# Turning the column results of the forward transform on the vector engine instead of the tensor engine

## The chip, the cores and the metric

The kernel runs on one core of one Trainium2 chip. The metric is device microseconds (us) of that core. Everything is computed in fp32.

## What is computed

The input x is 32 images of 32 channels of 128 x 128. Two layers follow each other, each of them "x plus something of the normalised x":

```python
def _gn(v, G=16, eps=1e-5):            # per image, groups of two channels
    g = v.reshape(B_, G, C_ // G, H_, W_)
    m = mean(g, (2, 3, 4)); s = var(g, (2, 3, 4))
    return ((g - m) / sqrt(s + eps)).reshape(v.shape)

# layer 0: five Newton-Schulz steps towards a matrix square root, 1024 matrices of 128 x 128
Y = A / norm(A); Z = I
for _ in range(5):
    T = 0.5 * (3.0 * I - Z @ Y); Y = Y @ T; Z = T @ Z
x = x + Y * sqrt(norm(A))              # A = _gn(x)

# layer 1: a spectral convolution with 32 x 32 modes at two corners
f = fftn(_gn(x), axes=(2, 3)).real
top = einsum('bixy,ioxy->boxy', f[:, :, :32, :32], weights1)
bot = einsum('bixy,ioxy->boxy', f[:, :, -32:, :32], weights2)
x = x + ifftn(zeros with top and bot in place).real
```

The change lies in the forward transform of layer 1, the real part of a two-dimensional Fourier transform cut to 64 rows of modes by 32 columns of modes.

## The kernel before, in words

Layer 0 works on 256 groups of four channels (`b` is the image, `g` the group in it). Each group is a lane, a generator (`newton`, L400) that yields between its steps; up to nine lanes are under way at once, and the main loop (L997) takes one step of each in every round. A step is mostly one set of four products 128 x 128 x 128 on the tensor engine (`products`, L304) into one PSUM bank, and one instruction that takes the bank out: the vector engine for q, v, w, t and xt (`plus`, L282, and L420), the scalar engine for y, m, mb and the final scaling (L276, L416). In most images (`is_far`) the two transposes of v go by the vector engine in 32 x 32 blocks (L373, tile `turn`) and through DRAM; the others go by the tensor engine (`transposed`, L310, against the identity). The eight PSUM banks turn in one pool (`bank`, L147).

Beside the lanes the loop takes steps of other queues: `preps` (statistics of the input), `norms`, `posts`, `specs`, `prods` and `backs` (mode products and inverse transform of images that are through). When a lane ends, `end` (L950) puts into `posts`:

- for each group `settle` (L426): it stores the result, folds columns w and -w into sums and differences on GpSimd (tile `fold`), and takes statistics on the vector engine (L437);
- for every four groups, twice an image and 64 times in all, `forward` (L443): products of the folds with cosines and sines (L455, L461, L467) give the column results of eight channels in one PSUM bank, whose four blocks of 32 partitions are 32 columns of modes, cosine or sine sum, for each of two sets of four channels. The scalar engine copies the bank out (`sw`, L472). In the next step the tensor engine transposes it (four transposes, L313 with tile `sw`), and the scalar engine copies the result, in two halves, into the image's tile `u` (L477), whose partitions are now the rows h;
- once an image `summed` (L485, the normalisation's statistics) and `spectrum` (L514): the row contraction, eight products an image, of 64 rows by 64 modes with 256 columns (L523, accumulated over the two sums s), a copy (tile `z`, L532), four transposes, the scaled spectrum (L541) and its store.

`u` has one buffer. The queue `posts` is stepped once in a round. What the engines' instruction streams look like is then decided by a planner that moves instructions by their readiness, except for those marked `kept`, which keep their order among themselves. At the end, when no lane is left, all queues are stepped without rounds between, and the last image's `forward`, `summed` and `spectrum` stand directly in the chain of work to the end of the kernel.

Of the kernel before, what the change touches and what calls it, by code (L numbers as in the profile page):

```python
# [29 lines left out]
F32 = mybir.dt.float32  # L30
# [6 lines left out]
P = 128  # L37
B = 32
C = 32
G = 16  # L40
# [15 lines left out]
K = 64  # L56
KK = 16
L = 32
# [3 lines left out]
T_FH = slice(64, 192)  # L62
# [6 lines left out]
def conv_preact_kernel(  # L69
# [8 lines left out]
    nc = tc.nc  # L78
# [347 lines left out]
    def settle(b, g, st, xt):  # L426

        kept(nc.sync.dma_start(out=mid[b][:, 4 * g : 4 * g + 4, :], in_=xt))
        if g % 2 == 0:
            folds[b, g // 2] = sets.tile([P, 8, P], F32, tag="fold", name=f"fold{b}_{g}", bufs=3)  # L430
        f = folds[b, g // 2][:, 4 * (g % 2) : 4 * (g % 2) + 4, :]
        for half, op in enumerate((ALU.add, ALU.subtract)):
            nc.gpsimd.tensor_tensor(  # L433
                f[:, :, 64 * half : 64 * half + 64], xt[:, :, 0:64], xt[:, :, 64:128], op
            )
        for j in range(2):
            nc.vector.bn_stats(  # L437
                st[:, 2 * g + j, :], xt[:, 2 * j : 2 * j + 2, :].rearrange("p c h -> p (c h)")
            )
        settled.append(rounds)  # L440
        yield

    def forward(b, q, u):  # L443


        yield
        fs = [folds.pop((b, 2 * q + i)) for i in range(2)]
        ps = bank()
        out = ps.rearrange("p j x -> p (j x)").rearrange("p (c h) -> p c h", h=64)
        cos, sin = (slice(T_FW.start + 32 * i, T_FW.start + 32 * i + 32) for i in range(2))  # L450

        for i in (1, 0):
            rows = slice(64 * i + 32, 64 * i + 64)
            kept(
                nc.tensor.matmul(  # L455
                    out[rows, :, 1:64], tab[:, sin], fs[i][:, :, 65:128], start=True, stop=True
                )
            )
            rows = slice(64 * i, 64 * i + 32)
            kept(  # L460
                nc.tensor.matmul(out[rows], tab[:, cos], fs[i][:, :, 0:64], start=True, stop=True)  # L461
            )

        for i in (1, 0):
            rows = slice(64 * i + 32, 64 * i + 64)
            kept(
                nc.tensor.matmul(  # L467
                    out[rows, :, 0], tab[:, cos], fs[i][:, :, 64], start=True, stop=True
                )
            )  # L470
        sw = sp.tile([P, 4, P], F32, tag="sp", name="sw", bufs=2)
        nc.scalar.copy(sw, ps)  # L472
        yield
        ps = transposed(sw)
        for i in range(2):
            c = 8 * q + 4 * i
            nc.scalar.copy(  # L477
                u[:, :, :, c : c + 4].rearrange("h s l c -> h (s l) c"),
                ps[:, :, 64 * i : 64 * i + 64].rearrange("h c m -> h m c"),
            )  # L480
        yield

    scales = {}
# [1 line left out]
    def summed(b, st):  # L485

        ms, _, d = yield from moments(st, "b")
        yield

        q = small.tile([P, G], F32, tag="b_qs", name=f"b_qs{b}")  # L490
        nc.vector.tensor_reduce(q, d, AX.X, ALU.add)
        qr = small.tile([P, 8, G], F32, tag="b_qr", name=f"b_qr{b}")
        nc.vector.tensor_copy(qr, q[:, None, :].to_broadcast([P, 8, G]))
        mr = small.tile([P, 2, G], F32, tag="b_mr", name=f"b_mr{b}")
        nc.vector.tensor_copy(mr, ms[:, None, :].to_broadcast([P, 2, G]))
        yield from pause
        pv = bank()[:, 0, :]
        nc.tensor.matmul(
            pv[:, 0:1], qr.rearrange("p l g -> p (l g)"), avg_v, start=True, stop=True
        )  # L500
        nc.tensor.matmul(
            pv[0:C, 1:2], mr.rearrange("p c g -> p (c g)"), avg_0, start=True, stop=True
        )
        v = small.tile([P, 2], F32, tag="b_v", name=f"b_v{b}")
        nc.vector.tensor_scalar(v[:, 0:1], pv[:, 0:1], 1.0, EPS, ALU.mult, ALU.add)
        nc.vector.tensor_copy(v[0:C, 1:2], pv[0:C, 1:2])
        yield
        s = root(v[:, 0:1], 1, "b_r", 256.0)
        r = small.tile([P, 1], F32, tag="b_inv", name=f"b_inv{b}")
        nc.vector.reciprocal(r, s)  # L510
        scales[b] = v, r
        yield

    def spectrum(b, u):  # L514


        uv = u.rearrange("h s (t e l) c -> h s e t (l c)", e=2, l=4)
        ps = [bank() for _ in range(2)]
        for s in range(2):
            for i in range(2):  # L520
                for e in range(2):
                    rows = slice(64 * i, 64 * i + 64)
                    nc.tensor.matmul(  # L523
                        ps[i][64 * e : 64 * e + 64, 0:2, :],
                        tab[rows, T_FH.start + s * K : T_FH.start + (s + 1) * K],
                        uv[rows, s, e],
                        start=(s == 0),
                        stop=(s == 1),
                    )
        z = sp.tile([P, 4, P], F32, tag="sp", name="z", bufs=2)  # L530
        for i in range(2):
            nc.scalar.copy(  # L532
                z.rearrange("p t (l i c) -> p (t l) i c", i=2, c=G)[:, :, i, :],
                ps[i].rearrange("p a x -> p (a x)")[:, 0:256].rearrange("p (m c) -> p m c", c=G),
            )
        yield
        v, r = scales.pop(b)
        ps = transposed(z)
        spec = sp.tile([P, 4, P], F32, tag="sp", name=f"spec{b}", bufs=2)
        spec = spec.rearrange("p a x -> p (a x)").rearrange("p (k q t) -> p k q t", q=4, t=8)  # L540
        nc.scalar.activation(  # L541
            spec.rearrange("p k q t -> p t (k q)"),
            ps.rearrange("p t (e k) -> p (t e) k", e=2),
            AF.Identity,
            scale=r,
        )
        nc.vector.scalar_tensor_tensor(  # L547
            spec[0:C, 0, 0, 0:1], v[0:C, 1:2], r[0:C], spec[0:C, 0, 0, 0:1], ALU.mult, ALU.add
        )
        yield  # L550
        i, j = where[b]
        if i == len(xs):

            for e, t in enumerate(diags):
                for l4 in range(4):
                    rows = slice(32 * l4, 32 * l4 + 32)
                    copy = nc.scalar.copy if l4 % 2 else nc.vector.tensor_copy
                    copy(  # L558
                        t.rearrange("p (m b l f) -> p m b l f", b=2, l=4, f=4)[rows, :, j, l4, :],
                        spec[rows, 8 * e : 8 * e + 8].rearrange("p k q (h f) -> p (k q h) f", f=4),  # L560
                    )
            yield
            return
        kept(
            nc.sync.dma_start(
                out=xs[i][:, :, j, :].rearrange("k p m -> p k m"),
                in_=spec.rearrange("p (k e) q t -> p k (e q t)", e=KK // xs[i].shape[0]),
            )
        )
        yield  # L570
# [379 lines left out]
    def end(b, g, xt):  # L950

        if g == 0:
            u = up.tile([P, 2, L, G], F32, tag="u", name=f"u{b}")
            st = small.tile([P, G, 6], F32, tag="b_st", name=f"b_st{b}", bufs=2)
            ended[b] = (u, st)
        u, st = ended[b]
        posts.append(settle(b, g, st, xt))
        if g == C // 4 - 1:
            posts.append(then(summed(b, st)))
        if g % 4 == 3:  # L960
            posts.append(forward(b, g // 4, u))
        if g == C // 4 - 1:
            posts.append(last(b, u))
# [33 lines left out]
    while todo or any(lanes) or posts or specs or prods or backs:  # L997
# [3 lines left out]
        for i in range(LANES):  # L1001
# [5 lines left out]
            if lanes[i] is None and todo and room and rounds >= due:  # L1007
# [3 lines left out]
                b, g = todo.pop(0)  # L1011
# [33 lines left out]
def _table():  # L1045

    import numpy as np

    k = np.concatenate([np.arange(32), np.arange(96, 128)]).reshape(4, KK).T.reshape(K)
    n = _order()  # L1050
    row = 2 * np.pi * (np.outer(n, k) % P) / P
    col = 2 * np.pi * (np.outer(n, np.arange(L)) % P) / P
    t = np.zeros((P, T_COLS))
    t[:, T_FW] = np.concatenate([np.cos(col), np.sin(col)], 1)
    half = np.concatenate([np.cos(row), -np.sin(row)], 1)[0:64]
    half[0] = np.concatenate([k % 2 == 0, k % 2 == 1])
    t[:, T_FH] = np.tile(half, (2, 1))
    half = np.concatenate([np.cos(row)[0:64], np.sin(row)[0:64]])
    half[0], half[64] = k % 2 == 0, -(k % 2)
    t[:, T_IH] = np.tile(half.T, (2, 1))  # L1060
    t[:, T_IW] = np.tile(np.concatenate([np.cos(col).T, np.sin(col).T], 1) / (P * P), (4, 1))
    return t.astype(np.float32)
# [37 lines left out]
```

## Time and profile before

| | |
|---|---|
| three runs of the kernel before | 3098.29, 3114.35, 3108.08 us |
| median | 3108.08 us |
| span of the profiled execution (first to last instruction; the profile states no other time of it) | 3098.6 us |
| TensorE (PE) busy | 2948.7 us, 95% |
| weight loads (PEld) busy | 2828.6 us, 91% |
| VectorE (DVE) busy | 2340.0 us, 76% |
| ScalarE (ACT) busy | 1704.0 us, 55% |
| GpSimd (POOL) busy | 1998.0 us, 64% |
| DMA | 636.78 MB, 206 GB/s over the span |

The profile is of one execution. A group of instructions is one source line on one engine with one pair of tiles; its "busy" counts time that overlaps with its neighbours once, and its "mean ns" is that of one instruction from start to end, so count times mean exceeds busy where instructions overlap. Every fp32 product shows as two MATMUL records: the four products of a lane's step are x8, one set of four transposes is x4. A timeline's second column is the duration of a merged stretch; the difference between the starts of two neighbours on one engine is the slot that the first one takes.

### The profile page before, as it was taken

How to read it: one execution, taken by the hardware profiler on the slowest of the kernel's cores; microseconds unless marked ns; L12 is line 12 of the kernel's file. 1: busy time of each engine (PE TensorE's matmuls, PEld its weight loads, DVE VectorE, ACT ScalarE, POOL GpSimd, SP SyncE). 2: the span in 40 equal slices, each digit the busy share in tenths (PEclk: the TensorE clock that was granted, in tenths of full speed). 3: DMA queues.
4: the chain of work that ended last, by engine and by line, in shares of the span. 5: the costliest groups of instructions: out<-in, count | busy, mean ns of one | idle time of the engine just before them, and what ended most of it. 6: DMA issues, size and time to landing. Idle time of an engine off the chain costs nothing. (4 is left out here: it accounts for less than half of the span.)

```text
span 3098.6 us, 79471 instructions
## 1 busy us (share of the span) xinstructions
PE 2948.7 (95%) x29760; PEld 2828.6 (91%) x29760; DVE 2340.0 (76%) x5178; ACT 1704.0 (55%) x4153; POOL 1998.0 (64%) x2312
## 2 busy tenths in 40 slices
PE   6999999999999999999999999999999998999994
PEld 6899999999999999999999998998899988899983
DVE  6788887888888787788877555788778766878654
ACT  3566556666665665666654444555454544555552
POOL 3567677677776666677665434768677764777453
PEclk9999999999999999999999999999999999999996
DMA  4576676666666666676743466667676876766666
GB/s 130 164 216 207 202 217 211 210 213 214 212 209 208 209 207 183 201 212 208 219 146 100 143 217 214 226 228 235 206 250 209 269 233 211 236 208 204 194 218 221
DMA packets 475150, 636.78 MB, mean 206 GB/s; under 512 B 97040, under 2 KB 255248, under 8 KB 474768
## 3 DMA queue, kind: packets, MB, share of 16 engines
q1 hardware_dynamic: 361872, 425.88, 42.8%
q10 hardware_dynamic: 112896, 205.83, 21.7%
q8 instruction: 237, 3.88, 0.5%
q14 instruction: 145, 1.19, 0.1%
HBM read 402.42 MB, written 229.11 MB: 204 GB/s over the span
## 5 line engine op out<-in xcount | busy, mean ns | idle before, releaser
L388 POOL TENSOR_TENSOR w<-w,r 128x512 f32<-128x512 f32 x288 | 366.3, 1276 | 324.3 <-DMA w<-turn 274.8
L307 PE MATMUL ps<-w,v 128*128 128x128 f32 x4096 | 554.6, 279 | 18.0 <-DVE w L282 7.7
L341 ACT ACTIVATE b<-b,a_off,a_scr 128x128 f32<-128x128 f32 x1024 | 468.7, 490 | 154.6 <-issue 48.1
L307 PE MATMUL ps<-y,q 128*128 128x128 f32 x4096 | 527.0, 277 | 6.2 <-ACT d L893 2.1
L307 PEld LDWEIGHTS ps<-w,v 128*128 128x128 f32 x4096 | 504.0, 194 | 25.1 <-POOL w L388 11.0
L307 PEld LDWEIGHTS ps<-y,q 128*128 128x128 f32 x4096 | 490.5, 193 | 9.6 <-issue 2.6
L433 POOL TENSOR_TENSOR fold<-xt 128x256 f32<-128x256 f32 x512 | 363.8, 731 | 204.5 <-DVE xt L420 192.2
L282 DVE SCALAR_TENSOR_TENSOR q<-ps,eye 128x512 f32<-128x512 f32 x512 | 348.0, 680 | 156.8 <-PE ps L307 151.5
L827 POOL TENSOR_TENSOR yt<-yt,d 128x512 f32<-128x512 f32 x248 | 311.2, 1282 | 153.7 <-ACT d L893 116.0
L301 POOL TENSOR_TENSOR r<-mb,eye 128x512 f32<-128x512 f32 x112 | 142.7, 1274 | 311.3 <-ACT mb L276 298.8
L348 POOL TENSOR_SCALAR x<-xt,a_nm,a_sc 128x128 f32<-128x128 f32 x736 | 322.7, 451 | 19.5 <-DVE a_n L231 19.5
L416 ACT ACTIVATE y<-ps,a_t_s 128x128 f32<-128x128 f32 x1024 | 291.4, 367 | 58.1 <-PE ps L307 57.6
L202 DVE BATCH_NORM_STATS2 a_st<-xs 128x6 f32<-128x128 f32 x1024 | 229.2, 278 | 108.7 <-DMA xs<-in_xt 107.9
L307 PE MATMUL ps<-m,q 128*128 128x128 f32 x2048 | 276.4, 278 | 8.1 <-DVE q L282 5.2
L307 PE MATMUL ps<-x,b 128*128 128x128 f32 x2048 | 277.0, 279 | 6.8 <-POOL x L348 5.6
L307 PE MATMUL ps<-m,mb 128*128 128x128 f32 x2048 | 276.7, 279 | 6.6 <-ACT d L893 4.3
L307 PE MATMUL ps<-x,q 128*128 128x128 f32 x2048 | 277.8, 279 | 3.3 <-DVE q L282 1.6
L307 PE MATMUL ps<-y,t 128*128 128x128 f32 x2048 | 275.1, 277 | 2.1 <-DVE t L282 2.0
L276 ACT ACTIVATE t<-ps 128x512 f32<-128x512 f32 x256 | 152.3, 595 | 223.1 <-PE ps L307 214.4
L307 PE MATMUL ps<-q,t 128*128 128x128 f32 x2048 | 274.9, 278 | 0.0
L373 DVE STREAM_TRANSPOSE turn<-v 128x512 f32<-128x512 f32 x288 | 262.0, 910 | 4.6
L307 PEld LDWEIGHTS ps<-m,q 128*128 128x128 f32 x2048 | 251.6, 193 | 10.7 <-DVE q L282 5.8
(148 smaller groups left out, 5768.2 us busy)
## 6 DMA issues: line engine op xcount, KB each, us to landing
turn<-turn SPq DMA_DIRECT2D x288, 256.0 KB
b<-in_x ACTq DMA_DIRECT2D x256, 256.0 KB
xt<-in_xt ACTq DMA_DIRECT2D x256, 256.0 KB
xs<-in_xt ACTq DMA_DIRECT2D x256, 256.0 KB
mid<-xt SPq DMA_DIRECT2D x256, 256.0 KB
yt<-mid SPq DMA_DIRECT2D x128, 512.0 KB
out<-yt SPq DMA_DIRECT2D x120, 512.0 KB
w<-turn SPq DMA_DIRECT2D x144, 256.0 KB
```

What stands on the lines that cost most here:

```text
L202: nc.vector.bn_stats(st[:, 4 * i + c, :], tiles[i][:, c, :])
L276: nc.scalar.mul(t, ps, f)
L282: nc.vector.scalar_tensor_tensor(s, ps, f, t, ALU.mult, ALU.add)
L301: nc.gpsimd.tensor_tensor(r, mb, eye, ALU.add)
L307: nc.tensor.matmul(ps[:, j, :], lhsT[:, j], rhs[:, j], start=True, stop=True)
L341: nc.scalar.activation(t, x, AF.Identity, bias=offset[:, c], scale=scale[:, c])
L348: nc.gpsimd.tensor_scalar(m[:, j, :], xt[:, j, :], nm[:, c // 2 : c // 2 + 1], sc[:, c : c + 1], ALU.add, ALU.mult,)
L373: nc.vector.transpose(blocks(t), v.rearrange(form, b=4))
L388: nc.gpsimd.tensor_tensor(w, w, r, ALU.add)
L416: nc.scalar.mul(y[:, j, :], py[:, j, :], sn[:, c : c + 1])
L433: nc.gpsimd.tensor_tensor(f[:, :, 64 * half : 64 * half + 64], xt[:, :, 0:64], xt[:, :, 64:128], op)
L827: engine.tensor_tensor(yh, yh, d, op)
```

## The change

`forward` no longer copies the bank to `sw`, transposes it on the tensor engine and copies it to `u`. One instruction of the vector engine reads the whole bank in PSUM (128 x 512) and writes it to `u`, each 32 x 32 block transposed. Since blocks stay in their partitions, `u` has another layout: a block of partitions holds one of the two sums for 32 of the 64 rows, and the other 32 rows lie elsewhere in the free dimension. `spectrum` therefore contracts, as before, over 64 partitions, but these are now 32 rows of the cosine sum and 32 rows of the sine sum at once, in two accumulated passes `a` over the two sets of rows; the table `T_FH` is put in the same order. The 256 columns that each product streams are read from `u` in runs of four floats (l), 16 bytes each, where they were runs of 64 floats. The count and sizes of these products are unchanged. `forward` has one yield less. The order of the channels in an image changes with it; statistics, their copies, the copies to `z` and the weights' layout on the host follow.

```diff
 settle:
         for j in range(2):
+            at = 8 * (g // 2 % 2) + 4 * (g // 4) + 2 * (g % 2) + j
             nc.vector.bn_stats(
-                st[:, 2 * g + j, :], xt[:, 2 * j : 2 * j + 2, :].rearrange("p c h -> p (c h)")
+                st[:, at, :], xt[:, 2 * j : 2 * j + 2, :].rearrange("p c h -> p (c h)")
             )
 forward:
-        sw = sp.tile([P, 4, P], F32, tag="sp", name="sw", bufs=2)
-        nc.scalar.copy(sw, ps)
-        yield
-        ps = transposed(sw)
-        for i in range(2):
-            c = 8 * q + 4 * i
-            nc.scalar.copy(
-                u[:, :, :, c : c + 4].rearrange("h s l c -> h (s l) c"),
-                ps[:, :, 64 * i : 64 * i + 64].rearrange("h c m -> h m c"),
-            )
+        nc.vector.transpose(
+            u[:, q].rearrange("p c a l -> p (c a l)"), ps.rearrange("p j x -> p (j x)")
+        )
         yield
 summed:
-        qr = small.tile([P, 8, G], F32, tag="b_qr", name=f"b_qr{b}")
-        nc.vector.tensor_copy(qr, q[:, None, :].to_broadcast([P, 8, G]))
-        mr = small.tile([P, 2, G], F32, tag="b_mr", name=f"b_mr{b}")
-        nc.vector.tensor_copy(mr, ms[:, None, :].to_broadcast([P, 2, G]))
+        qr = small.tile([P, 4, G, 2], F32, tag="b_qr", name=f"b_qr{b}")
+        nc.vector.tensor_copy(qr, q[:, None, :, None].to_broadcast([P, 4, G, 2]))
+        mr = small.tile([P, G, 2], F32, tag="b_mr", name=f"b_mr{b}")
+        nc.vector.tensor_copy(mr, ms[:, :, None].to_broadcast([P, G, 2]))
 spectrum:
-        uv = u.rearrange("h s (t e l) c -> h s e t (l c)", e=2, l=4)
+        uv = u.rearrange("p q c a (t e l) -> p a e t (q c) l", e=2, l=4)
         ps = [bank() for _ in range(2)]
-        for s in range(2):
+        for a in range(2):
             for i in range(2):
                 for e in range(2):
                     rows = slice(64 * i, 64 * i + 64)
                     nc.tensor.matmul(
                         ps[i][64 * e : 64 * e + 64, 0:2, :],
-                        tab[rows, T_FH.start + s * K : T_FH.start + (s + 1) * K],
-                        uv[rows, s, e],
-                        start=(s == 0),
-                        stop=(s == 1),
+                        tab[rows, T_FH.start + a * K : T_FH.start + (a + 1) * K],
+                        uv[rows, a, e],
+                        start=(a == 0),
+                        stop=(a == 1),
                     )
         z = sp.tile([P, 4, P], F32, tag="sp", name="z", bufs=2)
         for i in range(2):
             nc.scalar.copy(
-                z.rearrange("p t (l i c) -> p (t l) i c", i=2, c=G)[:, :, i, :],
-                ps[i].rearrange("p a x -> p (a x)")[:, 0:256].rearrange("p (m c) -> p m c", c=G),
+                z.rearrange("p t (l i c) -> p t l i c", i=2, c=G)[:, :, :, i, :],
+                ps[i].rearrange("p a x -> p (a x)")[:, 0:256].rearrange(
+                    "p (t c l) -> p t l c", c=G, l=4
+                ),
             )
 end:
-            u = up.tile([P, 2, L, G], F32, tag="u", name=f"u{b}")
+            u = up.tile([P, 2, 8, 2, L], F32, tag="u", name=f"u{b}")
 _table:
     half[0] = np.concatenate([k % 2 == 0, k % 2 == 1])
+    half = half.reshape(2, 32, 2, K).transpose(2, 1, 0, 3).reshape(64, P)
     t[:, T_FH] = np.tile(half, (2, 1))
```

The host's reordering of the weights, before the launch, is the rest of the diff.

More of the change, by code (lines that the diff above doesn't have):

```diff
@@ L498, in summed @@
         nc.tensor.matmul(
-            pv[:, 0:1], qr.rearrange("p l g -> p (l g)"), avg_v, start=True, stop=True
+            pv[:, 0:1], qr.rearrange("p l g c -> p (l g c)"), avg_v, start=True, stop=True
         )
         nc.tensor.matmul(
-            pv[0:C, 1:2], mr.rearrange("p c g -> p (c g)"), avg_0, start=True, stop=True
+            pv[0:C, 1:2], mr.rearrange("p g c -> p (g c)"), avg_0, start=True, stop=True
         )
@@ L1079 @@
     w = np.stack([np.asarray(inputs[f"L1_conv_weights{i}"]) for i in (1, 2)])
-    w = w.reshape(2, G, 2, 2, 4, 4, 2, KK, 2, 4, 4).transpose(7, 10, 2, 1, 8, 0, 6, 9, 3, 5, 4)
+    w = w.reshape(2, 2, 2, 8, 2, 4, 4, 2, KK, 2, 4, 4)
+    w = w.transpose(8, 11, 2, 1, 3, 9, 0, 7, 10, 4, 6, 5)
     arrays = {
```

## The prediction

> **What bounds the kernel now.** I read the page first: busy time of each engine, and the slices.
>
> ```profile
> PE 2948.7 (95%) x29760; PEld 2828.6 (91%) x29760; DVE 2340.0 (76%) x5178; ACT 1704.0 (55%) x4153; POOL 1998.0 (64%) x2312
> ...
> PE   6999999999999999999999999999999998999994
> ```
>
> The tensor engine is all but full from the second slice to the last but one. A busy tensor engine can still be waiting inside, so I next read busy time by stretch (columns: stretch, its length, PE, PEld, DVE, ACT, POOL, clock, DMA share, GB/s):
>
> ```profile
> 500.00:1000.00 500.00, 497.12 (x4495) 483.23 (x4494) 412.15 (x936) 307.88 (x761) 354.50 (x392) 1.00 0.69 211
> 1000.00:1500.00 500.00, 491.59 (x4407) 477.30 (x4406) 410.15 (x913) 300.78 (x744) 348.57 (x387) 0.99 0.68 206
> ...
> 2000.00:2500.00 500.00, 482.03 (x4740) 459.01 (x4738) 397.71 (x851) 263.81 (x662) 364.57 (x426) 0.99 0.69 231
> 2500.00:3000.00 500.00, 466.08 (x6147) 441.96 (x6146) 345.56 (x707) 264.17 (x609) 300.39 (x358) 0.98 0.67 213
> ```
>
> Up to 2000 us PE is idle in at most 2% of the time and DVE is next with up to 82%; after that PE has 4 to 7% of gaps. The timeline of PE around one `forward` tells whether busy means full:
>
> ```profile
> 1035.95 1.06 PE L307 MATMUL ps<-y,q 128*128 128x128 f32 x8
> 1036.85 0.60 PE L313 MATMUL ps<-ident,sw 128*128 128x128 f32 x4
> 1037.29 0.94 PE L307 MATMUL ps<-w,v 128*128 128x128 f32 x7
> ```
>
> From start to start the eight records of a step take 0.90 us and the four transposes 0.44 us: 0.11 us a record, one on the heels of the other. So PE is the bound, and time taken off its queue there comes off the kernel.
>
> [...]
>
> **The change part by part.** The rows concerned, of the groups with shapes apart (busy us, mean ns, idle before and releaser):
>
> ```profile
> L313 PE MATMUL ps<-ident,sw 128*128 128x128 f32 x256 | 39.7, 279 | 5.6 <-ACT sw L472 5.6
> L472 ACT COPY sw<-ps 128x512 f32<-128x512 f32 x64 | 37.5, 585 | 43.4 <-PE ps L467 38.0 <-POOL x L348 1.9 <-DVE a_st L202 1.6
> L477 ACT COPY u<-ps 128x256 f32<-128x256 f32 x128 | 41.4, 379 | 29.5 <-PE ps L313 29.5
> L523 PE MATMUL ps<-u,tab 64*64 64x256 f32 x512 | 35.9, 397 | 0.0
> L373 DVE STREAM_TRANSPOSE turn<-v 128x512 f32<-128x512 f32 x288 | 262.0, 910 | 4.6
> ```
>
> *Removed from PE:* 64 sets of four transposes. The group's 39.7 us counts the ends of records that overlap the next ones; the slot is what the queue loses: 64 x 0.44 = 28.2 us. I also compared the order of instructions in the two built programs: PE's stream is the same but for the 64 sets, so nothing else moves on it.
>
> Up to 2000 us (176 of the 256 transposes, by stretch) the saving is whole. In the last third (80 transposes, 20 sets, 8.8 us) PE often waits for others; I take half: 28.2 - 4.4 = 23.8 us.
>
> *Removed waits:* PE waited for `sw` 5.6 us. Part of this would only pass to the next wait: I count half, 2.8 us.
>
> *Removed from ACT:* 37.5 + 41.4 = 79 us of copies. ACT is at 55%, so I count nothing for it; it can only help (PE's waits for ACT's m, mb, y and t are 11 us in all). If ACT had become late elsewhere, those 11 us are the most it returns.
>
> *Added to DVE:* 64 transposes of 128x512 out of PSUM. The two durations of `turn` have a reason that the timeline shows:
>
> ```profile
> 1032.49 0.67 DVE L282 SCALAR_TENSOR_TENSOR v<-ps,m 128x512 f32<-128x512 f32 x1
> 1033.20 0.71 DVE L373 STREAM_TRANSPOSE turn<-v 128x512 f32<-128x512 f32 x1
> ...
> 1035.36 0.69 DVE L282 SCALAR_TENSOR_TENSOR v<-ps,x 128x512 f32<-128x512 f32 x1 [0.88 <-PE ps L307]
> 1036.09 1.13 DVE L373 STREAM_TRANSPOSE turn<-v 128x512 f32<-128x512 f32 x1
> ```
>
> The first is a lane's second quartic, which reads v in runs of 32 floats; the second is the first quartic, which reads with a step of four floats. The new one reads and writes without gaps, so the fast one is its nearest row; PSUM as a source costs 0.67 to 0.69 us for v itself. I take 0.71 us, with 0.64 (the least of `turn`) and 1.13 as ends: 64 x 0.71 = 45.4 us, and DVE goes from 2340 to 2385 us, 77%.
>
> What is queued behind it: DVE's next q, t, v or w, which PE waits for. It stands in DVE's stream where a statistic (L202, 0.28 us, nobody's hurry) stood before, and it waits there for L467, PE's last fold product. While it waits PE itself is not past the folds, so nobody is held; only its own 0.71 us can be. The lanes give PE other work meanwhile: PE's waits for DVE's lane results are 30 us in all now, against 2340 us of DVE work. I let a tenth of the new work through to PE: 4.5 us; bounds 0 and 45.4.
>
> *Moved, same price:* L523 keeps count and columns; its slot for an image is 1.03 us (1009.26 to 1010.29), 33 us in all. I take the short runs as free[...]; bounds 0 and once more the streaming, which I estimate from the records: 273 ns for 128 columns and 376 ns for 256 are 0.80 ns a column; 16 records of 256 columns with four side by side are 4 x 0.206 = 0.82 us an image, 26 us in all. The `z` copies now read PSUM with a step, as L477 did at 379 ns like the plain copies: nothing. Statistics and small copies keep their counts: nothing. DMAs: none added or moved but for places of a few `mid` stores on SP's queue, whose sum is the same.
>
> *The end:* there the chain is bare.
>
> ```profile
> 3037.70 0.22 PE L467 MATMUL ps<-fold,tab 128*32 128x8 f32 x4
> 3038.65 1.12 PE L313 MATMUL ps<-ident,sw 128*128 128x128 f32 x4 [0.73 <-ACT sw L472]
> 3039.56 0.45 PE L172 MATMUL ps<-b_ms,avg_mean 128*128 128x16 f32 x2
> ```
>
> L172, which opens the statistics that the spectrum waits for, queues behind the transposes. Afterwards it follows the folds at about 3038.0, and DVE takes its result right after the new transpose (3038.05 + 0.71 = 3038.8) instead of at 3040.04: 1.3 us.
>
> *Sum:* -23.8 - 2.8 - 1.3 + 4.5 = -23.4 us on the profiled 3098.6 us, so a span of 3075. The median of the runs is 9.5 us above that span; I carry the difference over: 3108.1 - 23.4 = 3084.7 us, 0.75% less. Its own range, from the shares chosen above: 3073 (all of 28.2 + 5.6 + 1.3 comes through, nothing is lost to DVE) to 3094 (23.8 + 1.3, no wait saved, a quarter of the new DVE work, 11 us, passed on to PE).
>
> **The rivals.** *A: the vector engine becomes the bound (slower).* Speaks for it: 82% busy in the full stretches, and w and q lead the lane waits of PE. Against: it has 18% idle there and most of its own waits are for PE. Price: each transpose delays PE by its 0.71 us and by half of the folds' slot (1.02 us from 30.95 to 31.97) in which DVE used to do statistics: 64 x 1.22 = 78 us, less 28.2 and 1.3, is +48.6: 3157 us. It decides from 29.5/64 = 0.46 us of PE delay per transpose. *B: the short runs slow L523.* Doubled streaming gives 26 us back, the waits stay: 3111 us. For it: the step of four floats cost `turn` 0.4 us on DVE[...]. *C: the saving becomes waits* for lanes that are late anyway; only the waits and the end, and a quarter of the slots (7 us), remain: 3108.1 - 11 = 3097 us. Against: 99% busy PE in the stretches with most sets.
>
> **Chances.** Forecast 0.68, A 0.14, B 0.09, C 0.09. About 0.5% (15.5 us) is what a measurement of this kernel can tell from no change: faster means under 3092.5, slower over 3123.6. B and C count as the same; so faster 0.68, same 0.18, slower 0.14. The range must leave out at most 2 in 10: 3064 to 3116 takes in the forecast, B and C and leaves out A.
>
> **What would show it.** Right: no `ident,sw` rows; PE about 28 us of slots less and still over 98% busy before 2000 us; 64 new STREAM_TRANSPOSE at about 0.7 us; L523 at 376 ns; PE's waits for DVE below 45 us; L172 within 0.5 us of the last fold. Wrong: L523 records of 550 ns or more (B), PE's waits for DVE's q, w and v grown by tens of us (A), PE's busy share fallen before 2000 us with the same span (C).

## The result and the profile after

| | before | changed |
|---|---|---|
| median of six runs, us | 3104.19 (3098.29 to 3114.35) | 3077.16 (3070.69 to 3084.34) |
| span of the profiled execution, us | 3098.6 | 3078.2 |

The ratio is 0.991 with a 95% interval of 0.9893 to 0.9927: the kernel is 28 us faster, 23 to 33 by the interval. The spans of the two profiled executions differ by 20.4 us only. That of before was one of the shortest: three more runs put the median of before at 3104.2, not 3108.1. So what is read off the pair of traces is a little small, and sizes below come from the timed runs where there are any.

First the changed kernel's page, busy time of each engine:

```profile
PE 2922.9 (95%) x29504; PEld 2801.7 (91%) x29504; DVE 2374.3 (77%) x5242; ACT 1634.7 (53%) x3961; POOL 2001.8 (65%) x2312
```

PE lost 256 records and 25.8 us of busy time, ACT 69 us, and DVE gained 34 us, less than 64 x 0.70, since neighbours on DVE overlap at their ends by some 0.07 us (in the timeline below, `u` begun at 1023.49 ends at 1024.16, and t begins at 1024.09). By stretch, columns as before:

```profile
500.00:1000.00 500.00, 497.06 (x4489) 483.00 (x4488) 421.12 (x959) 296.74 (x730) 358.45 (x396) 1.00 0.68 211
1000.00:1500.00 500.00, 494.69 (x4459) 480.43 (x4452) 423.30 (x944) 296.18 (x727) 357.87 (x395) 1.00 0.68 210
1500.00:2000.00 500.00, 488.30 (x5164) 463.44 (x5162) 341.35 (x793) 244.01 (x581) 274.87 (x351) 0.99 0.57 179
...
2500.00:3000.00 500.00, 462.40 (x6068) 437.70 (x6067) 350.05 (x706) 252.81 (x578) 295.53 (x350) 0.97 0.67 215
```

PE is as full as before between 500 and 1500 us: the time taken out was filled with the next products, nothing opened up in its place. DVE went from 82% to 84 or 85% there. From 1500 to 2000 us PE is 97.7% busy (98.0% before), so the prediction's sign of over 98% up to 2000 us was narrowly missed there.

The new instruction and the products that read its result, groups with shapes apart:

```profile
L472 DVE STREAM_TRANSPOSE u<-ps 128x512 f32<-128x512 f32 x64 | 44.9, 701 | 10.4 <-PE ps L468 10.4
L517 PE MATMUL ps<-u,tab 64*64 64x256 f32 x512 | 36.5, 397 | 1.3 <-ACT d L889 1.3
```

701 ns for a transpose out of PSUM, and the products' mean is 397 ns as it was, although they now read runs of four floats. The same `forward` whose folds began at 1030.95 us before, in time order on PE and DVE:

```profile
1022.28 0.22 PE L468 MATMUL ps<-fold,tab 128*32 128x8 f32 x4
1022.43 1.16 PE L307 MATMUL ps<-q,t 128*128 128x128 f32 x8
1023.49 0.67 DVE L472 STREAM_TRANSPOSE u<-ps 128x512 f32<-128x512 f32 x1
1023.86 1.06 PE L307 MATMUL ps<-x,b 128*128 128x128 f32 x8
1024.09 0.65 DVE L282 SCALAR_TENSOR_TENSOR t<-ps,eye 128x512 f32<-128x512 f32 x1
```

The transpose starts 1.21 us after the last fold products begin, behind other work of DVE, and DVE's next result for a lane, t, follows 0.60 us after it began. PE goes on with other lanes without a pause. And the end of the kernel:

```profile
3017.91 0.28 PE L468 MATMUL ps<-fold,tab 128*32 128x8 f32 x4
3018.13 0.61 PE L172 MATMUL ps<-b_ms,avg_mean 128*128 128x16 f32 x2
3018.28 0.72 DVE L472 STREAM_TRANSPOSE u<-ps 128x512 f32<-128x512 f32 x1 [2.07 <-PE ps L468]
3018.92 0.14 DVE L174 TENSOR_SCALAR b_nm<-ps 128x16 f32<-128x16 f32 x1
...
3020.99 1.98 PE L517 MATMUL ps<-u,tab 64*64 64x256 f32 x16
```

Before, the first product of the spectrum stood here:

```profile
3042.22 1.98 PE L523 MATMUL ps<-u,tab 64*64 64x256 f32 x16
```

L172 follows the folds at once. From the start of the last fold product to the first product of the spectrum it is 3.08 us (3017.91 to 3020.99), against 4.52 us before (3037.70 to 3042.22). Of these 1.4 us the end of this pair of executions shows nothing: the fold products just ahead took 0.8 us longer in the profiled execution of the changed kernel, and its lead, 20.6 us when they begin (3016.23 against 3036.83), is 20.4 us at the end.

### The profile page after: what moved, and what is told of

Its sections match the earlier page's. It is cut to its first block, busy times and chain, and to the rows that moved or that the text cites. A ratio compares the mean times of both kernels' runs of the same rounds, so it can differ in the third digit from the quotient of the medians.

```text
span 3078.2 us, 78788 instructions
## 1 busy us (share of the span) xinstructions
PE 2922.9 (95%) x29504; PEld 2801.7 (91%) x29504; DVE 2374.3 (77%) x5242; ACT 1634.7 (53%) x3961; POOL 2001.8 (65%) x2312
## 4 chain that ended last, share of the span: by engine, by line
PE 76%; DMA 10%; DVE 8%; ACT 1%; POOL 1%; issue 1%; SPq 1%; ACTq 0%; DVEq 0%; POOLq 0%
PE ps L307 62%; PE ps L313 6%; DMA xs<-in_xt 4%; PE ps L877 2%; PE ps L456 2%; DMA w<-turn 1%; PE ps L855 1%; DVE a_st L202 1%; PE ps L517 1%; PE ps L604 1%; DVE yt L894 1%; DMA diag<-in_wk 1%; DVE v L282 1%; PE ps L674 1%; DMA or<-od 1%
## 5 line engine op out<-in xcount | busy, mean ns | idle before, releaser
L307 PE MATMUL ps<-w,v 128*128 128x128 f32 x4096 | 550.8, 278 | 15.8 <-POOL w L388 8.1
L307 PE MATMUL ps<-y,q 128*128 128x128 f32 x4096 | 532.1, 278 | 5.4 <-ACT d L889 2.1
L307 PEld LDWEIGHTS ps<-w,v 128*128 128x128 f32 x4096 | 500.5, 193 | 22.8 <-POOL w L388 9.6
L307 PEld LDWEIGHTS ps<-y,q 128*128 128x128 f32 x4096 | 495.3, 194 | 8.5 <-ACT d L889 2.3
L282 DVE SCALAR_TENSOR_TENSOR q<-ps,eye 128x512 f32<-128x512 f32 x512 | 347.9, 680 | 147.7 <-PE ps L307 141.6
L348 POOL TENSOR_SCALAR x<-xt,a_nm,a_sc 128x128 f32<-128x128 f32 x736 | 324.9, 453 | 20.1 <-DVE a_n L231 20.1
L307 PE MATMUL ps<-m,q 128*128 128x128 f32 x2048 | 277.5, 279 | 13.4 <-DVE q L282 9.3
L307 PE MATMUL ps<-m,mb 128*128 128x128 f32 x2048 | 276.1, 278 | 6.0 <-ACT d L889 4.3
L307 PE MATMUL ps<-x,b 128*128 128x128 f32 x2048 | 274.5, 277 | 6.8 <-POOL x L348 5.6
L307 PE MATMUL ps<-x,q 128*128 128x128 f32 x2048 | 276.1, 278 | 4.5 <-DVE q L282 2.9
L307 PE MATMUL ps<-y,t 128*128 128x128 f32 x2048 | 275.7, 278 | 3.0 <-DVE t L282 2.0
L307 PE MATMUL ps<-q,t 128*128 128x128 f32 x2048 | 274.9, 278 | 0.0
L307 PEld LDWEIGHTS ps<-m,q 128*128 128x128 f32 x2048 | 252.1, 194 | 16.6 <-DVE q L282 10.4
L276 ACT ACTIVATE y<-ps 128x512 f32<-128x512 f32 x256 | 152.5, 596 | 215.8 <-PE ps L307 202.7
```

The source lines that it names most:

```text
L276: nc.scalar.mul(t, ps, f)
L282: nc.vector.scalar_tensor_tensor(s, ps, f, t, ALU.mult, ALU.add)
L307: nc.tensor.matmul(ps[:, j, :], lhsT[:, j], rhs[:, j], start=True, stop=True)
L348: nc.gpsimd.tensor_scalar(m[:, j, :], xt[:, j, :], nm[:, c // 2 : c // 2 + 1], sc[:, c : c + 1], ALU.add, ALU.mult,)
```

## The experiments

The theory is the prediction's: the change takes 64 x 0.44 us out of the queue of a full tensor engine, and everything that it puts elsewhere is nearly free. The rivals: the scalar engine's relief is what helps; the vector engine is close to being the bound; short runs cost the tensor engine time. Ratios are to the kernel before, run beside each of them; the changed kernel was not run again beside them. "To changed" is the difference of the two ratios times 3105 us. It is good to 6 to 9 us either way, from the two intervals together.

| run | ratio, 95% interval | to changed |
|---|---|---|
| the change | 0.9910 (0.9893 to 0.9927) | |
| e1, transposes left out of before | 0.9908 (0.9888 to 0.9927) | -1 us |
| e2, scalar copies back | 0.9894 (0.9874 to 0.9914) | -5 us |
| e3, tensor transposes back | 1.0001 (0.9989 to 1.0014) | +28 us |
| e4, five vector transposes | 0.9965 (0.9950 to 0.9980) | +17 us |
| e7, nine vector transposes | 1.0210 (1.0187 to 1.0233) | +93 us |
| e12, one more per settle | 0.9951 (0.9936 to 0.9966) | +13 us |
| e11, two more per settle | 1.0005 (0.9992 to 1.0017) | +29 us |
| e9, tensor work early | 1.0019 (1.0005 to 1.0032) | +34 us |
| e8, tensor work late | 1.0003 (0.9991 to 1.0015) | +29 us |
| e10, runs of two floats | 0.9905 (0.9886 to 0.9925) | -2 us |
| e5, runs of one float | 0.9975 (0.9965 to 0.9985) | +20 us |

### Whose time was it: tensor or scalar engine?

The kernel before without its 64 sets of transposes:

```diff
-        ps = transposed(sw)
         for i in range(2):
             c = 8 * q + 4 * i
             nc.scalar.copy(
                 u[:, :, :, c : c + 4].rearrange("h s l c -> h (s l) c"),
-                ps[:, :, 64 * i : 64 * i + 64].rearrange("h c m -> h m c"),
+                sw[:, :, 64 * i : 64 * i + 64].rearrange("h c m -> h m c"),
             )
```

> The kernel before with only the 64 sets of tensor-engine transposes left out: the scalar engine copies sw straight to u, so the column results are not turned and the spectral part of the output is wrong; the scalar engine keeps its 79 us or a little more. Theory (the gain is the slots of the transposes on the tensor engine, 28 us, and nothing else): about as fast as the changed kernel, 23 to 30 us under the kernel before. Rival (the gain comes from the relief of the scalar engine and of its waits): no gain, within 8 us of the kernel before.

The whole gain is there, although the scalar engine is busier than before: its copies now read `sw` in SBUF with a step and take 654 ns instead of 379. ACT is busy for 1737.6 us, against 1704.0 before.

```profile
L476 ACT COPY u<-sw 128x256 f32<-128x256 f32 x128 | 77.7, 654 | 1.9 <-DMA turn<-turn 0.5 <-ACT sw L472 0.5
```

The converse, the changed kernel with the scalar engine's load put back:

```diff
             u[:, q].rearrange("p c a l -> p (c a l)"), ps.rearrange("p j x -> p (j x)")
         )
+        sw = sp.tile([P, 4, P], F32, tag="sp", name="sw", bufs=2)
+        flat = sw.rearrange("p j x -> p (j x)")
+        nc.scalar.copy(flat, u[:, q].rearrange("p c a l -> p (c a l)"))
+        yield
+        for i in range(2):
+            half = flat[:, 256 * i : 256 * i + 256]
+            nc.scalar.copy(half, u[:, q, 4 * i : 4 * i + 4].rearrange("p c a l -> p (c a l)"))
```

> The changed kernel with the three copies of the scalar engine added again for each forward (one of 128x512 and two of 128x256, from u to a scratch tile that nobody reads; about 80 to 100 us of scalar-engine work in all). Theory: no more than 4 us slower than the changed kernel, so 22 to 30 us under the kernel before. Rival (scalar-engine relief is the gain): back to the kernel before, within 8 us.

ACT is back at 1706.6 us, and nothing is lost (-5 us is within the noise). And the changed kernel with four transposes back on the tensor engine:

```diff
             u[:, q].rearrange("p c a l -> p (c a l)"), ps.rearrange("p j x -> p (j x)")
         )
+        yield
+        dead = bank()
+        for j in range(4):
+            nc.tensor.transpose(dead[:, j, :], u[:, q].rearrange("p c a l -> p (c a l)")[:, P * j : P * j + P], ident)
```

> The changed kernel with four tensor-engine transposes added again for each forward, a step later, of u into a bank that nobody reads; the scalar engine's copies stay out. Theory: 64 x 0.44 us = 28 us come back up to 2000 us of the run and little after it: 20 to 28 us slower than the changed kernel, so within 8 us of the kernel before. Rival (scalar-engine relief): as fast as the changed kernel, 23 to 30 us under the kernel before.

The kernel is back at the time of before. Its group shows that not all of the 28 us need be slots, since PE here sometimes waits for DVE's `u`, 12.6 us in all (the kernel before waited 5.6 us for `sw`):

```profile
L478 PE MATMUL ps<-ident,u 128*128 128x128 f32 x256 | 39.6, 278 | 12.7 <-DVE u L472 12.6
```

The three runs agree: what the transposes took on the tensor engine counts (e1 is 1 us under the changed kernel, e3 28 us over it), and scalar-engine time cost nothing here (e2 puts 72 us of it back and is 5 us under the changed kernel, within the noise). The rival of the scalar engine's relief has fallen. How the 28 us divide between the slots and the waits for `sw` or `u` these runs don't tell. Another rival is that each set also takes a turn of a PSUM bank; the next runs bear on it.

### What does tensor-engine time cost early and late?

Sixteen transposes were added to each `forward` of eleven images, late (`b >= 21`) or early (`4 <= b < 15`):

```diff
         )
+        if b >= 21:
+            yield
+            dead = bank()
+            flat = u[:, q].rearrange("p c a l -> p (c a l)")
+            for j in range(16):
+                j %= 4
+                nc.tensor.transpose(dead[:, j, :], flat[:, P * j : P * j + P], ident)
         yield
```

> The same sixteen transposes added to each forward of the images 4 to 14, also 22 forwards and 39 us in slots, between about 500 and 1350 us. Theory (there the tensor engine is the bound): all of it, 35 to 45 us over the changed kernel. If the lanes had slack there: under 25 us.

> The changed kernel with sixteen tensor-engine transposes (into a bank that nobody reads) added to each forward of the images from 21 on, which run after about 1900 us: 22 x 16 x 0.11 = 39 us more in slots. The prediction's step says that half of such work comes through there: 19 us over the changed kernel. If the last third is bound by something else altogether, as the constant lead of the changed kernel there suggests: under 8 us. If it is tensor-bound after all: 35 us or more.

One set of sixteen in the early run, on PE:

```profile
713.64 1.91 PE L481 MATMUL ps<-ident,u 128*128 128x128 f32 x16
715.38 1.06 PE L307 MATMUL ps<-m,q 128*128 128x128 f32 x8
```

Its slot is 1.74 us, 0.109 us a transpose, 38 us for 22 sets. Early, 34 of 38 us came through (27 to 40 by the intervals; a bit under what was expected, within the noise), late 29 (22 to 35). For the late third that is more than the half that the prediction took and less than all; some three quarters is the best estimate. Late and early cannot be told apart by these times. The traces say where the rest went: against the changed kernel's, PE's busy time grew by 38.9 us (late) and 37.8 us (early), while its waits fell by 9.7 and 5.6 us, so some of the added products ran when PE would have waited. The near-constant lead after 2000 us, which I had read out of the pair of traces, did not mean that tensor-engine time is free there.

The banks don't explain the cost: the early run takes 22 turns of a bank more and e3 takes 64, yet the early run, with 352 added transposes against 256, costs no less (34 us against 28).

### How close is the vector engine to being the bound?

Four more transposes behind the first one, or, with `range(8)`, eight:

```diff
             u[:, q].rearrange("p c a l -> p (c a l)"), ps.rearrange("p j x -> p (j x)")
         )
+        sw = sp.tile([P, 4, P], F32, tag="sp", name="sw", bufs=2)
+        for _ in range(4):
+            nc.vector.transpose(
+                sw.rearrange("p j x -> p (j x)"), u[:, q].rearrange("p c a l -> p (c a l)")
+            )
```

> The changed kernel with four more vector-engine transposes of 128x512 in each forward (from u into a scratch tile that nobody reads): 256 x 0.70 = 180 us more on the vector engine, standing together behind the first. Theory (a tenth of new vector-engine work reaches the tensor engine): 18 us slower than the changed kernel, range 5 to 40, so still below or level with the kernel before. Rival A (the vector engine is about to become the bound, the change lives on its last slack): well over half of the 180 us, 90 us or more over the changed kernel, 65 us or more over the kernel before.

> The changed kernel with eight more vector-engine transposes in each forward (512 x 0.70 = 358 us more on the vector engine, which then is busy for about 86% of the span and over 90% between 500 and 1500 us). Theory (a tenth of new vector-engine work reaches the tensor engine, in proportion): twice what four more cost, 37 us over the changed kernel. Rival A (a knee: from some load on the vector engine is the bound): well over that, 80 us or more over the changed kernel.

Four more cost 17 us, a tenth of their 178 us. Eight more cost 93 us, a quarter of their 355 us, where a cost in proportion, 37 us, had been the theory's answer: above some point between four and eight the cost grows faster than the work. Where PE waits in the run with nine:

```profile
engine line waited for: us in total, times, longest us
PE ps L497 <- DVE b_qr L492: 23.1, 15, 4.3
PE ps L307 <- DVE q L282: 18.3, 17, 4.8
PE ps L307 <- POOL w L388: 15.9, 10, 3.9
...
PE ps L313 <- DVE v L282: 13.3, 13, 2.9
```

PE's waits for `b_qr`, a small copy at the end of the statistics of `summed`, grew most, from 4.4 us in the changed kernel to 23.1 us. Waits are not the whole cost. This execution is 87 us longer than the changed kernel's; PE waits 193.6 us in all against 141.6, and the other 35 us are busy time for the same number of products, at a mean granted clock of 0.977 against 0.982. What made them longer is open.

The nine transposes do not stand together in DVE's stream as the expectations assume. One `forward` of this run, DVE only:

```profile
1092.51 0.70 DVE L472 STREAM_TRANSPOSE u<-ps 128x512 f32<-128x512 f32 x1
1093.13 0.65 DVE L282 SCALAR_TENSOR_TENSOR v<-ps,m 128x512 f32<-128x512 f32 x1
1093.71 0.69 DVE L477 STREAM_TRANSPOSE sw<-u 128x512 f32<-128x512 f32 x1
1094.32 0.67 DVE L373 STREAM_TRANSPOSE turn<-v 128x512 f32<-128x512 f32 x1
1094.91 0.67 DVE L477 STREAM_TRANSPOSE sw<-u 128x512 f32<-128x512 f32 x1
1095.51 0.65 DVE L282 SCALAR_TENSOR_TENSOR t<-ps,eye 128x512 f32<-128x512 f32 x1
```

The planner has put other work between them: the nine take 9.0 us from the first to the end of the last (median of the 64 forwards; 5.0 us for the five of e4), with eight other instructions in between, four of which take lane results out of PSUM. So both runs tried a crowd of transposes within a few microseconds, not a burst in which nothing else is done. Is it the load, then, or where the work stands? The same work, spread over the `settle` steps, two in each (or one, for half of it):

```diff
                 st[:, at, :], xt[:, 2 * j : 2 * j + 2, :].rearrange("p c h -> p (c h)")
             )
+        sw = sp.tile([P, 4, P], F32, tag="sp", name="sw", bufs=2)
+        for _ in range(2):
+            nc.vector.transpose(
+                sw.rearrange("p j x -> p (j x)"), xt.rearrange("p c h -> p (c h)")
+            )
```

> The changed kernel with the same 512 additional vector-engine transposes as in the run with nine turns, but spread: two in each of the 256 settle steps (of xt, into a scratch tile that nobody reads) instead of eight behind each of the 64 forwards. If the 92 us that the eight cost come from the vector engine's load: again 80 us or more over the changed kernel. If they come from the length of the burst, 5.6 us in which no result is taken out of PSUM: half or less, under 45 us.

> The changed kernel with 256 additional vector-engine transposes, one in each settle step, the same work as in the run with five turns (18.6 us over the changed kernel). If load decides: 18 us again. If burst decides: under 9 us, hardly to be told from the changed kernel.

The spread run has DVE busier than any other, yet PE is almost full:

```profile
500.00:1000.00 500.00, 494.60 (x4440) 479.35 (x4439) 466.32 (x1041) 293.09 (x722) 355.59 (x393) 1.00 0.69 210
```

93% of the stretch on DVE (91% in the run with nine), and the cost is 29 us for 356 us of work, 8%, a third of what the crowd cost. So the load alone does not make the dear case. In the traces PE waits 33.4 us less than in the run with nine, about what it waits less for `b_qr` (4.3 against 23.1 us) and for the lanes' results from DVE (33.9 against 48.7 us) together. Whether the crowding counts or the place, ahead of the statistics of `summed`, stays open: this run changes both. For half of the work the two answers can't be told apart: 13 us spread, 17 us in crowds of five.

### Are short runs free, and from where not?

That runs of four floats cost nothing was an assumption of the prediction; it had no row of before to show it. Two runs go further down: the spectrum's products with runs of one float, and of two, both at a step of four floats:

```diff
-        uv = u.rearrange("p q c a (t e l) -> p a e t (q c) l", e=2, l=4)
+        uv = u.rearrange("p q c a l -> p (q c a l)").rearrange("p (n m) -> p m n", m=4)
...
-                        uv[rows, a, e],
+                        uv[rows, 2 * a + e],
```

> The changed kernel, but the spectrum's products read u with a step of four floats (16 bytes), runs of one, instead of runs of four; they contract the wrong elements, so the spectral part of the output is not the reference's; count and columns as before. Rival B's mechanism[...]: the records of the spectrum's products grow from 376 ns to about 580 ns and the kernel becomes up to 26 us slower than the changed one. Other answer (the fp32 stream, 0.8 ns a column, is slow enough for any step): 376 ns stay and the time is that of the changed kernel within 5 us.

Of runs of two, two things were thought possible: they take as long as runs of four, or something between runs of four and runs of one.

```diff
-        uv = u.rearrange("p q c a (t e l) -> p a e t (q c) l", e=2, l=4)
+        uv = u.rearrange("p q c a l -> p (q c a l)").rearrange("p (n m k) -> p m n k", m=2, k=2)
...
-                        uv[rows, a, e],
+                        uv[rows, a, 128 * e : 128 * e + 128],
```

> The changed kernel, but the spectrum's products read u in runs of two floats with a step of four (8 of every 16 bytes); they contract the wrong elements, so the spectral part of the output is not the reference's. Runs of four left the records at 376 ns, runs of one made them 628 ns. [...] 376 ns and the changed kernel's time within 5 us. [...] 450 to 550 ns and 8 to 15 us slower.

The group of the products, first with runs of one:

```profile
L517 PE MATMUL ps<-u,tab 64*64 64x256 f32 x512 | 65.3, 632 | 1.3 <-ACT d L889 1.3
```

and with runs of two:

```profile
L517 PE MATMUL ps<-u,tab 64*64 64x256 f32 x512 | 37.7, 405 | 1.3 <-ACT d L889 1.3
```

Runs of one take the mean record from 397 to 632 ns, and 20 us of the kernel; runs of two take it to 405 ns, 8 ns more than runs of four, and nothing that the time shows (-2 us). So the cost that rival B feared is there for runs of one, 235 ns a record, but the change, with runs of four, pays none of it: 397 ns, as before. Why one float at a time is slow, and what runs of four would cost at other steps, these runs don't show.

## Why the prediction was right, point by point

The predicted time, 3084.7 us, was 7.5 us too high. Half of that, 3.9 us, is the median of before, which three more runs lowered from 3108.1 to 3104.2; the rest is the sum, 23.4 us for a measured 27 (medians) or 28 (ratio). The mechanism was right; that the sum came so near is in part luck, since its shares were chosen, not measured, and errors of opposite sign cancel in it.

- *Slots on PE, 23.8 us.* Right in kind (e1 and e3), probably a little small: some three quarters, not half, of the work in the last third comes through (e8). With 8.8 x 0.75 there and the 19.4 us before it, the term is 26.0 us, or 24 if the early share is e9's 34 of 38.
- *Waits for `sw`, 2.8 us.* Not confirmed. The wait is gone, but PE's waits for other engines add up to 123.7 us before and 123.6 us after: those for DVE's `b_qr` (1.5 to 4.4 us) and of L307 for q (7.9 to 12.3) grew. With the waits for DMA (10.5 and 17.1 us) and the few for which the profile shows no cause they are 135.9 and 141.6 us. So in this pair PE has 25.8 us less of busy time and 5.7 us more of waits, which makes 20.1 of the 20.4 us between the spans. This step of the sum was better put at nothing.
- *Scalar engine, nothing.* Right (e2: -5 us, within the noise).
- *Vector engine, 45.4 us of work, a tenth of it, 4.5 us, through to PE.* The work is right: 64 transposes at 701 ns. The tenth was a guess. Of the runs with more transposes three bear it out, 7% (e12), 8% (e11) and 10% (e4), and one doesn't, 26% (e7). For the change's own 64 it is an estimate from these: PE's waits for q, t, v, w and xt rose from 30.9 to 33.9 us, and e1, which has none of the transposes, differs by 1 us, give or take 8. That the transpose takes the place of a statistic is only in part so: directly behind it stands a lane result (L282 or L420) in 34 of the 64 cases. That its wait for the folds holds nobody fits the one timeline shown.
- *Short runs, nothing.* Right: 376 ns as the median and 397 ns as the mean, before and after. It had been assumed, not shown. The estimate of what they could cost, 26 us, was near e5's 20 us for runs of one.
- *The end, 1.3 us.* 1.4 us from the last fold product on, though the pair of spans does not show it. The sum counts some 0.6 us of it twice: the last set's slot and its wait for `sw` (0.44 and 0.73 us) stand with a half each in the first two terms too.

With those sizes the sum is 26.0 + 1.4 less 3 to 4, so 23 to 24 us, inside the interval of 23 to 33 but at its lower end. What makes up the rest, if it is anything, these runs can't tell.

Of the rivals, A's point (0.46 us of PE delay for each transpose) was far off: by the estimate above, 3 to 4 us in 64, it is 0.06 us each, and e1 leaves room for 0.13 us. B is refuted by the records of L517 (397 ns on the mean, as before), and C by the time itself, with e1 and e3 for its reason.

## What to carry to other kernels

The tensor engine was nearly full here, 98 to 99% busy between 500 and 1500 us, and the edit was worth 28 us (23 to 33): about the 28.2 us of slots, start to start, that it took out of that engine's queue, not the 71 us that 256 records of 279 ns add up to. Work put on the engines with more idle time, spread out, came to less than a tenth of its duration: nothing of 72 us on the scalar engine (53% busy in the changed kernel), 13 of 177 us and 29 of 356 us on the vector engine (77%). The same vector work cost three times as much with eight transposes behind each `forward` as with two in each `settle`, 93 us against 29. So where added work stands has to be tried along with how much it is, and its place has to be read from the trace: the planner had mixed with other work what the source has in one loop. Where a new layout shortens the runs that a product reads, try the run length by itself: here records with runs of four floats took 397 ns, with runs of two 405 and with runs of one 632.

## What the runs showed of the hardware

- The spectrum's fp32 products (256 columns) took 397 ns a record on the mean with their streamed operand read from SBUF in runs of 64 floats (before) and in runs of four (changed), 405 ns in runs of two at a step of four floats (e10), and 632 ns in runs of one at that step (e5).
- A 128x512 fp32 block transpose on the vector engine took 701 ns out of PSUM and 693 to 696 ns out of SBUF, without gaps in the reads, so PSUM as the source cost at most 8 ns more.
- A scalar-engine copy of 128x256 with the same steps took 379 ns out of PSUM before, and 654 ns out of SBUF in e1.
